# A graph layer with a residual and a norm: 32 instead of 24 hot regions, 1524 instead of 1402 edges a later part, rows weighted in place, sums made part by part

## The chip, the cores and the metric

The kernel runs on one core of a Trainium2 chip. The metric is the device time of one execution in microseconds (us). The kernel before was run three times for its time; a further execution was recorded by the hardware profiler, and all durations of instructions are from that one.

## The reference

A layer of a graph network on 12,500 nodes with 128 features each, and 412,500 edges (200,000 pairs in both directions and one loop at each node), sorted by their target `dst`; all float32:

```python
theta = x[dst] - x[src]
w = jax.nn.sigmoid(jax.nn.relu(theta @ W1 + b1) @ W2 + b2)
agg = jax.ops.segment_sum(w * theta, dst, num_segments=n_nodes)
indeg = jax.ops.segment_sum(jnp.ones((E, 1)), dst, num_segments=n_nodes)
out = _layernorm(x + agg + indeg * (x @ W4 + b4))
```

The sources are random: for each edge a row of 128 floats has to be fetched from a random place. The targets are sorted, so the edges of a part of the list belong to a narrow window of nodes, and a sum by target is a product with a one-hot matrix over that window.

## The kernel before

**Tables.** In 14 chunks (`table_chunk`, L724 to L757) the kernel writes to DRAM the rows z = [x W1 | x] (1 KB a node, by way of buffers `zbuf`) and u = x W4 + b4. The x-rows of a chunk come by way of the buffers `wx`.

**Early parts.** The first 26 parts (`PLAIN`) have 1024 edges each. Every part takes eight indirect gathers of 128 rows (`gather`, L362 to L390, the DMA at L373, issued by POOL; the first eight parts gather from x, the rest from z). POOL carries a short pause between two gathers (`engine_nop`).

**Later parts.** All other edges, 385,876, are cut into 275 parts of 1402 (`CE`) and a tail of 326. Such a part has 1024 gathered slots and 384 hot slots. A hot slot needs no gather: the x-rows of 24 (`HR`) regions of 256 nodes stay in SBUF (`tabs`), each region gives 16 slots a part, and its rows are picked by a product with a one-hot matrix. `place` (L473 to L685) decides which edges of a part become hot: for a set of 64 parts at a time it works on VectorE, region by region, on rows of 702 columns (`WL`) with L548, L552, L553 and L555, and then moves the other edges together in eight steps (L644 to L651). It is a generator: a few of its steps run in each part, as many as a credit allows (`spend`, L1285), beginning some parts before the set is needed. The five sets are 64, 64, 64, 64 and 20 parts; the first is placed during the tables and early parts.

**What a later part does**, with x the source and y the target side:
- PE spreads the target rows: y (L878 in `spread_pair`, for both parts of a block of two), from a one-hot `oh` that ACT makes (L837, L838; `one_hot`, for both parts of a block).
- DVE makes the logits on the gathered rows: subtract (L908), relu times W2 (L913), sum over features (L919), and the one-hot `ow` (L888) by which the sums are made.
- ACT makes the gate by sigmoid (`open_gate`, L925), and again with the counts into the weighted rows (`gate_sums`, L931, L935). DVE weighs four of the eight tiles of 128 rows (L953), ACT the others (L960). The weighted rows go to buffers `wx`, apart from the gathered ones.
- For hot rows, ACT makes the one-hot `of` out of `hot_src` (`hot_tiles`, L996 twice and L998), PE picks the rows (`hot_products`, `pd`, L1010), ACT copies them to `xT` (`hot_out`, L1024). This goes by fetches, each for four regions and eight parts; six fetches serve eight parts (`LEADS`). `hot_rows` (L1043 to L1060) transposes the rows of both parts of a block (L1051), multiplies them by -W1 (L1054) and adds the targets (L1058); DVE makes their logits (L1068), ACT weighs them (L1079), DVE makes their one-hot `owh` (L1083).
- `add_block` (L1121 to L1132) sums both parts of a block at once in PSUM (`pa`, L1101), hot rows too, over a window of 96 nodes (`WB`), and carries the sum on to the next block by a shift matrix (`sh`, L1095, L1096).
- `total`, `finish`, `own` and `normalize` (L1134 to L1200) add the residual and norm the finished rows.

**What sets the order.** In the later parts PE, DVE and ACT run in the order in which the code issues (`IN_ORDER`), written out in `part` (L1363 to L1430). The ring of gather buffers has seven places; part s issues the gathers of part s + 3 (`spread_ahead`, L1356), and the first of the eight waits for the newest PE product issued until then (`paced`), which is one of the part before. SP issues the loads of `hot_src`, window rows and outputs, POOL the gathers.

Of the kernel before, what the change touches and what calls it, by code (L numbers as in the profile page):

```python
# [9 lines left out]
F32 = mybir.dt.float32  # L10
# [10 lines left out]
P = 128  # L21
# [6 lines left out]
WB = 96  # L28
SW = 48
HALF = 64  # L30
AW = 130
G = 4
# [12 lines left out]
HR = 24  # L45
# [7 lines left out]
LEADS = (0, 1, 2, 4, 5, 6)  # L53
NU = 3
# [5 lines left out]
LAST = 121  # L60
LISTS = 2
S2 = P // LISTS
CE = 1402
# [6 lines left out]
PM = 53  # L70
BIG = 1 << 16
STEP = (PM + 1) * HOT
AREA = SW * STEP
# [6 lines left out]
def gnn_resnorm(  # L80
# [46 lines left out]
    assert HOT == 256 and PM == 53 and (HR + 1) * AREA < 1 << 24 and CE % LISTS == 0  # L127
# [165 lines left out]
    def constants():  # L293
# [21 lines left out]
        apart = const.tile([P, PM], F32, name="apart")  # L315
        nc.vector.tensor_scalar(apart, iota_row[:, :PM], float(HOT), None, op0=OP.mult)
# [3 lines left out]
        return nodes, (apart, most, area_c)  # L320


    wx_buf = [const.tile([P, K, AW], F32, name=f"wx{i}") for i in range(NW)]
    wxh_buf = [const.tile([P, SUB * HQ, AW], F32, name=f"wxh{i}") for i in range(2)]
    for t in wxh_buf:
        nc.vector.memset(t[:, :, D + 1:], 1.0)
    xT_all = const.tile([P, HX, HK], F32, name="xT")
# [10 lines left out]
    zbuf = [const.tile([P, K, 2 * D], F32, name=f"zbuf{i}") for i in range(NZ)]  # L338
# [6 lines left out]
    def filled(t, s):  # L345

        if s < NF:
            return t
        return t.rearrange("p (h j) d -> p h j d", h=2)[:, :, :JT, :]

    def rows_of(s):

        if s < NH:
            t = zbuf[s // 2].rearrange("p k d -> p (k d)")[:, (s % 2) * BE:(s % 2 + 1) * BE]
            return t.rearrange("p (k d) -> p k d", d=D)
        return zbuf[(s - NH + NX) % NZ]
# [116 lines left out]
    def place(i, scratch, es, ed, bb, dp):  # L473
# [7 lines left out]
        apart, most, area_c = hot_c  # L481
# [4 lines left out]
        v.tensor_scalar(c[:, 17:18], dp, -float(STEP), float(HR * AREA), op0=OP.mult, op1=OP.add)  # L486
# [17 lines left out]
        nc.scalar.activation(left[:, :HL], ed[:, :HL], AF.Identity, scale=float(STEP), bias=c[:, 17:18])  # L504
# [5 lines left out]
        for j in range(2):  # L510
# [26 lines left out]
        whole = WL // PM * PM  # L537
        v.tensor_tensor(
            left[:, :whole].rearrange("p (a m) -> p a m", m=PM),
            left[:, :whole].rearrange("p (a m) -> p a m", m=PM),  # L540
            apart.rearrange("p (o m) -> p o m", o=1).to_broadcast([P, WL // PM, PM]), op=OP.add)
        if whole < WL:
            v.tensor_add(left[:, whole:], left[:, whole:], apart[:, :WL - whole])
        yield "k"
# [25 lines left out]
        v.tensor_scalar(high, high, HOT.bit_length(), (1 << 13) - 1,  # L570
                        op0=OP.logical_shift_right, op1=OP.bitwise_and)
        v.tensor_scalar(high, high, float(-(-(1 << 16) // ((PM + 1) // 2))), None, op0=OP.mult)
        v.tensor_scalar(high, high, 16, None, op0=OP.logical_shift_right)
# [26 lines left out]
        NC = 4  # L600
        C = -(-WL // NC)
        assert 3 * C <= WL - HKL // 2 and 3 * C < 2 * P * G
        for j in range(NC):
            at = slice(j * C, min(j * C + C, WL))
            m = at.stop - at.start
            pw = scratch()[:, :2 * P * G]
            odd, count, far_on = pw[:, :m + 1], pw[:, C + 1:C + 1 + m], pw[:, 2 * C + 1:2 * C + 1 + m]
# [21 lines left out]
            v.tensor_mul(far_on, count, keep)  # L629
            v.tensor_scalar(keep, far_on, float(LAST), None, op0=OP.is_ge)  # L630
            v.scalar_tensor_tensor(move, keep, -float(P + LAST), far_on, op0=OP.mult, op1=OP.add)
            v.scalar_tensor_tensor(w[:, at], move, 24, w[:, at], op0=OP.logical_shift_left,
# [10 lines left out]
        assert SW + HKL < 2 * LAST and LAST < P - 1 and WL <= 2 * P * G  # L643
        for r, m in enumerate([1 << r for r in range(7)] + [LAST]):  # L644
            u = ep.tile([P, WL], I32, name="et" if r % 2 else "ew")
            bit = scratch().bitcast(I32)[:, :WL]
            v.tensor_scalar(bit, w, 7 - r, 31, op0=OP.logical_shift_left, op1=OP.arith_shift_right)
            v.scalar_tensor_tensor(u, bit, -1, w, op0=OP.bitwise_xor, op1=OP.bitwise_and)
            v.copy_predicated(u[:, :WL - m].bitcast(F32), bit[:, m:], w[:, m:].bitcast(F32))
            yield "m" if r < 7 else "z"  # L650
            w = u  # L651
# [35 lines left out]
    with tc.manual_schedule(engines={SP}), tc.tile_pool(name="work", bufs=2) as wp, tc.tile_pool(  # L687
# [28 lines left out]
        def table_load(c):  # L716
            n0, np_, m = chunks[c]
            xt = wx_buf[c % NW].rearrange("p k d -> p (k d)")[:, :BE]
            xt = xt.rearrange("p (t d) -> p t d", d=D)
            nc.scalar.dma_start(  # L720
                xt[:np_, :m, :], x[n0:n0 + np_ * m, :].rearrange("(p t) d -> p t d", t=m))
            return xt

        def table_chunk(c, xt):  # L724

            n0, np_, m = chunks[c]
            zt = zbuf[NX + c % 3]
# [139 lines left out]
        def spread_pair(b):  # L867

            ys = []
            for h in range(SUB):  # L870
                y = ps_y.tile([P, G, D], F32, name="y")
                parts[b * SUB + h]["y"] = [y]
                ys.append(y)
            for j in range(J):
                for h, y in enumerate(ys):
                    s = b * SUB + h
                    if j < pairs(s):
                        nc.tensor.matmul(y[:, j, :], parts[s]["oh"][:, j * P:(j + 1) * P], y_of(s),  # L878
                                         start=True, stop=True)

        def one_hot_w(s):

            (_, rel, _), i = set_of(s)
            n = pairs(s)
            parts[s]["ow"] = []
            for k0 in range(0, K if s < PLAIN else J, J):
                ow = wp.tile([P, J, WB], F32, name="ow", bufs=4)
                nc.vector.tensor_tensor(  # L888
                    ow[:, :n], iota_f.to_broadcast([P, n, WB]),
                    rel[:, k0:k0 + n, i:i + 1].to_broadcast([P, n, WB]), op=OP.is_equal)  # L890
                parts[s]["ow"].append(ow)

        def logits(s):
# [11 lines left out]
            n = pairs(s)  # L905
            half = h.rearrange("p (i k) d -> p i k d", i=2)[:, :, :n, :]
            yy = y[0][:, :n, :].rearrange("p (o k) d -> p o k d", o=1)
            nc.vector.tensor_sub(half, yy.to_broadcast([P, 2, n, D]), half)  # L908
            w2 = w2_b.rearrange("p (o d) -> p o d", o=1)
            n = K if s < NF else JT  # L910
            tiles = [slice(i, i + n) for i in range(0, K, J if n < K else K)]
            for at in tiles:
                nc.vector.scalar_tensor_tensor(  # L913
                    h[:, at, :], h[:, at, :], 0.0, w2.to_broadcast([P, n, D]),
                    op0=OP.max, op1=OP.mult)
            if s % SUB == 0:
                one_hot_w(s)
            for at in tiles:
                nc.vector.tensor_reduce(lg[:, at, 0], h[:, at, :], AX.X, OP.add)  # L919
            if s % SUB:  # L920
                one_hot_w(s)

        def open_gate(s):

            nc.scalar.activation(filled(gate[:, s % 2].rearrange("p (k e) -> p k e", e=1), s),  # L925
                                 filled(parts[s]["lg"], s), AF.Sigmoid, bias=b2_c)

        def gate_sums(s):

            wx = wx_buf[s % NW]  # L930
            nc.scalar.activation(filled(wx[:, :, D:D + 1], s), filled(parts[s]["lg"], s),  # L931
                                 AF.Sigmoid, bias=b2_c)
# [3 lines left out]

        def weigh(s):

            zs = rows_of(s)
            if s < PLAIN:  # L940
                wx = wx_buf[s % NW]
                for k in range(K):
                    nc.scalar.activation(wx[:, k, :D], zs[:, k, :] if s < NH else zs[:, k, D:],  # L943
                                         AF.Copy, scale=wx[:, k, D:D + 1])
# [3 lines left out]
            if s < NF:  # L948
                xs = zs[:, :KV, D:]
                w, wx = w[:, :KV], wx[:, :KV]  # L950
            else:
                xs, w, wx = filled(zs[:, :, D:], s), filled(w, s), filled(wx, s)
            nc.vector.tensor_tensor(wx, xs, w.to_broadcast(list(xs.shape)), op=OP.mult)  # L953

        def weigh_rest(s):

            if s < NF:
                wx = wx_buf[s % NW]
                for k in range(KV, K):
                    nc.scalar.activation(wx[:, k, :D], rows_of(s)[:, k, D:], AF.Copy,  # L960
                                         scale=wx[:, k, D:D + 1])
# [72 lines left out]
        def hot_y(b, h, q):  # L1034
            return blocks[b]["px"][:, h * P * G + q * P:h * P * G + (q + 1) * P]

        def hot_x(b, i):

            if i < G:
                return pz[:, i * P:(i + 1) * P]  # L1040
            return hot_y(b, i - G, HQ)
# [589 lines left out]
```

## Time and profile before

| | us |
|---|---|
| runs | 3891.53, 3894.61, 3896.50 |
| median | 3894.61 |
| profiled execution | 3877.69 |
| its span, first to last instruction | 3875.8 |
| granted TensorE clock, mean | 0.80 of full |
| one gather of 128 rows on POOL, mean of 2204 | 0.961 |

The profiled execution lies 0.4% below the median; a sum of durations is made against it and then moved to the median.

How to read the lines in the prediction: a row of the timeline is start, duration, engine, line, operation, output and inputs, count, and in brackets how long the engine stood before it and what released it ("remote" where no recorded end fits, "issue" where nothing in the profile was waited for). A row of the groups has the busy time and mean duration in ns behind the bar, then the idle time before these instructions by releaser. A row of the stages has the stretch, its length, and what the text names. PE is TensorE, PEld its weight loads, DVE VectorE, ACT ScalarE, POOL GpSimd, SP SyncE. L12 is line 12 of the kernel before.

### The profile page before, as it was taken

Reading aid. Unit: us, or ns where it says so; the run is one execution under the profiler, and the core shown is the slowest. Engines: PE = TensorE matmul, PEld = TensorE weight load, DVE = VectorE, ACT = ScalarE, POOL = GpSimd, SP = SyncE. Lnnn points to the kernel's source line nnn. Section 1 sums busy time; section 2 is a strip of 40 time slices with the busy share of each in tenths; the row PEclk is TensorE's granted clock in tenths of the full one; section 3 lists DMA queues with packets and bytes.
Section 4 is the critical chain, followed back from the end, with each engine's and each line's share of the span. In section 5 each row is a group of like instructions: output and inputs, shape, how many; then the busy total and the mean of one; then the engine's idle time right before and its main releaser. Section 6 shows DMA issues by size and latency. Waiting matters only on the chain.

```text
span 3875.8 us, 56094 instructions
## 1 busy us (share of the span) xinstructions
PE 2445.5 (63%) x15792; PEld 2080.0 (54%) x15792; DVE 2570.0 (66%) x5694; ACT 2136.0 (55%) x5542; POOL 2324.0 (60%) x2421
## 2 busy tenths in 40 slices
PE   6776566666666666666666666656666666666666
PEld 5555455555555555555555555555555555555555
DVE  6445257777775777777657777776577777765555
ACT  5454455555556555555555555555555555555554
POOL 5544436666666666666666666666666666666663
PEclk9786777778778787878888888788878887788887
DMA  7332224444444444444444434444444444444432
GB/s 265 116 106 76 76 76 112 113 110 115 112 113 120 113 113 113 114 112 112 113 119 113 113 112 111 114 111 112 113 113 112 114 113 114 112 112 112 113 108 71
DMA packets 259988, 437.36 MB, mean 113 GB/s; under 512 B 69817, under 2 KB 177800, under 8 KB 258132
## 3 DMA queue, kind: packets, MB, share of 16 engines
q0 software_dynamic: 114752, 312.11, 28.9%
q1 hardware_dynamic: 142946, 115.19, 11.0%
q10 hardware_dynamic: 1970, 6.40, 0.5%
q8 instruction: 127, 2.08, 0.2%
q14 instruction: 193, 1.58, 0.1%
HBM read 406.12 MB, written 27.33 MB: 112 GB/s over the span
## 4 chain that ended last, share of the span: by engine, by line
DVE 29%; another core or an unknown queue 23%; ACT 16%; issue 15%; PE 13%; POOL 2%; DMA 2%; DVEq 0%; SPq 0%; POOLq 0%; ACTq 0%
DVE zbuf L913 5%; DVE zbuf L908 5%; DVE lg L919 4%; DVE hh L1068 4%; ACT wxh L1079 3%; PE pa L1101 3%; ACT wx L960 3%; ACT of L996 2%; PE pd L1010 2%; POOL zbuf L373 2%; ACT of L998 2%; DVE ow L888 2%; ACT xT L1024 1%; DVE ew L555 1%
## 5 line engine op out<-in xcount | busy, mean ns | idle before, releaser
L373 POOL DMA_INDIRECT zbuf<-z,src_i x2204 | 2117.8, 961 | 1323.7 <-issue 497.2
L1010 PE MATMUL pd<-of,tabs 128*128 128x128 f32 (+1 forms) x3392 | 557.0, 330 | 779.3 <-ACT xT L1024 681.1
L1010 PEld LDWEIGHTS pd<-of,tabs 128*128 128x128 f32 x3392 | 523.6, 242 | 799.2 <-ACT xT L1024 696.5
L1101 PE MATMUL pa<-wx,ow 128*96 128x260 f32 (+1 forms) x2620 | 610.2, 386 | 31.1 <-issue 17.9
L908 DVE TENSOR_TENSOR zbuf<-y,zbuf 128x1024 f32<-128x1024 f32 (+1 forms) x276 | 336.3, 1218 | 338.9 <-remote 275.5
L996 ACT ACTIVATE of<-hot_src,nodes 128x512 f32<-128x512 f16 (+2 forms) x424 | 282.0, 701 | 503.8 <-remote 407.8
L1101 PEld LDWEIGHTS pa<-wx,ow 128*96 128x96 f32 x2620 | 419.1, 172 | 172.1 <-issue 40.0
L953 DVE TENSOR_TENSOR wx<-zbuf,fix 128x512 f32<-128x512 f32 x276 | 189.2, 686 | 399.7 <-ACT fix L925 381.5
L878 PE MATMUL y<-y,oh 64*128 64x128 f32 x2204 | 277.4, 362 | 264.2 <-issue 255.7
L878 PEld LDWEIGHTS y<-y,oh 64*128 64x128 f32 x2204 | 222.5, 252 | 309.0 <-issue 288.1
L960 ACT ACTIVATE wx<-zbuf,wx 128x128 f32<-128x128 f32 x1100 | 349.4, 388 | 0.0
L913 DVE SCALAR_TENSOR_TENSOR zbuf<-zbuf,fix 128x1024 f32<-128x1024 f32 (+1 forms) x277 | 336.5, 1215 | 10.6 <-DVE zbuf L908 0.6
L919 DVE TENSOR_REDUCE lg<-zbuf 128x8 f32<-128x1024 f32 (+1 forms) x277 | 334.7, 1209 | 4.7
L1068 DVE SCALAR_TENSOR_TENSOR hh<-px,w_r 128x128 f32<-128x128 f32 x828 | 240.1, 290 | 139.9 <-remote 113.7
L1054 PE MATMUL px<-wni,xT 128*128 128x128 f32 x1656 | 280.8, 321 | 60.3 <-issue 59.9
L1054 PEld LDWEIGHTS px<-wni,xT 128*128 128x128 f32 x1656 | 260.9, 238 | 68.9 <-issue 68.5
L1024 ACT ACTIVATE xT<-pd 128x512 f32<-128x512 f32 (+7 forms) x347 | 132.0, 415 | 297.5 <-remote 253.3
L1101 PE MATMUL pa<-wxh,owh 128*96 128x130 f32 x1656 | 227.3, 277 | 78.5 <-issue 76.9
L1101 PEld LDWEIGHTS pa<-wxh,owh 128*96 128x96 f32 x1656 | 204.5, 164 | 108.8 <-issue 93.3
L925 ACT ACTIVATE fix<-lg,b_c 128x8 f32<-128x8 f32 (+1 forms) x276 | 74.7, 271 | 325.1 <-issue 179.6
L373 POOL DMA_INDIRECT zbuf<-z,src x144 | 137.6, 955 | 144.3 <-ACT wx L943 98.2
L998 ACT ACTIVATE of<-of 128x1024 f32<-128x1024 f32 (+2 forms) x212 | 219.7, 1036 | 6.5
(266 smaller groups left out, 3885.5 us busy)
## 6 DMA issues: line engine op xcount, KB each, us to landing
zbuf<-z,src_i POOLq DMA_INDIRECT x2204
to_all<-off_d SPq DMA_DIRECT2D x276, 112.0 KB
hot_src<-hot_s SPq DMA_DIRECT2D x182, 128.0 KB
z<-zbuf SPq DMA_DIRECT2D x12, 1024.0 KB
xw<-in_x_dram SPq DMA_DIRECT2D x151, 48.0 KB
u<-u_d SPq DMA_DIRECT2D x151, 48.0 KB
out_dram<-o SPq DMA_DIRECT2D x151, 48.0 KB
y<-z SPq DMA_DIRECT2D x294, 24.0 KB
```

The costliest lines, as they stand in the source:

```text
L373: ins = nc.gpsimd.indirect_dma_start(out=rows_of(s)[:, k, :], out_offset=None, in_=z if s >= NH else x, in_offset=IndirectOffsetOnAxis(ap= ...
L878: nc.tensor.matmul(y[:, j, :], parts[s]["oh"][:, j * P:(j + 1) * P], y_of(s), start=True, stop=True)
L908: nc.vector.tensor_sub(half, yy.to_broadcast([P, 2, n, D]), half)
L913: nc.vector.scalar_tensor_tensor(h[:, at, :], h[:, at, :], 0.0, w2.to_broadcast([P, n, D]), op0=OP.max, op1=OP.mult)
L919: nc.vector.tensor_reduce(lg[:, at, 0], h[:, at, :], AX.X, OP.add)
L960: nc.scalar.activation(wx[:, k, :D], rows_of(s)[:, k, D:], AF.Copy, scale=wx[:, k, D:D + 1])
L996: nc.scalar.activation(of[:, t, :], hot_src[:, i % NU, :w], AF.Abs, bias=nodes[:, t:t + 1])
L998: nc.scalar.activation(of, of, AF.Relu, scale=-1.0, bias=1.0)
L1010: newest[0] = nc.tensor.matmul(to[:, q], tabs[:, g * RG + q, t, :], of[:, t, q], start=t == 0, stop=t == HT - 1)
L1054: nc.tensor.matmul(hot_y(b, h, q), xT[:, h, q * P:(q + 1) * P], wneg, start=False, stop=False, skip_group_check=True)
L1068: nc.vector.scalar_tensor_tensor(h, hot_y(b, *divmod(q, HQ)), 0.0, w2_r, op0=OP.max, op1=OP.mult, accum_out=lg[:, q, :])
L1101: newest[0] = nc.tensor.matmul(to if len(w.shape) == 3 else to[:, 0, :], one, w, start=first and i == 0, stop=last and i == len(terms) - 1)
```

## The change

- A later part has 1524 edges: 1024 gathered slots as before and 512 hot ones of 32 regions. The same edges make 253 full parts and a tail of 304; the sets of `place` are 64, 64, 64 and 62 parts. The tail's sums use the same code as a full part.
- Eight fetches instead of six serve eight parts, one a part; `hot_src` has four buffers instead of three.
- The window of a block is 112 instead of 96 nodes.
- The `wx` buffers go. A row of the gather ring is 260 floats instead of 256, and rows are weighted in place, with the gate and the count behind them. So a place of the ring comes free when PE has summed it. In the table phase the z rows leave from buffers of that pitch.
- Sums are made part by part: `add_part` (s - 1) in part s in place of `add_block`. Hot rows too: `products_ahead` (s + 1, s + 2) makes the hot products of the next part, in one PSUM tile `px`, and the y of the one after.
- In `part` the fetch step stands at the start instead of the end, and a part earlier or later as the diff shows; `one_hot` stands ahead of the logits; the steps of `place` are spent once, at the end of a part, with a credit of 3.0 instead of 2.1.
- `place` has a shorter sort key, without the part number `apart`, 32 rounds, and nine steps of moving in two halves each, on 763 columns.

```diff
-WB = 96
-SW = 48
+WB = 112
+SW = 56
+ZW = 2 * AW
...
-HR = 24
+HR = 32
...
-LEADS = (0, 1, 2, 4, 5, 6)
-NU = 3
+LEADS = (0, 1, 2, 3, 4, 5, 6, 7)
+NU = 4
...
-CE = 1402
+CE = 1524
...
-    wx_buf = [const.tile([P, K, AW], F32, name=f"wx{i}") for i in range(NW)]
...
-    zbuf = [const.tile([P, K, 2 * D], F32, name=f"zbuf{i}") for i in range(NZ)]
+    zbuf = [const.tile([P, K, ZW], F32, name=f"zbuf{i}") for i in range(NZ)]
...
+    def own_of(s):
+        if s < NH:
...
+        return ring(s)[:, :, D:D + AW]
...
-        apart, most, area_c = hot_c
+        most, area_c = hot_c
...
-        for r, m in enumerate([1 << r for r in range(7)] + [LAST]):
...
+        for r in range(MOVES):
+            m = 1 << r
+            u = ep.tile([P, WL], I32, name="ew" if r % 2 else "et")
+            for c0 in range(0, WL, C):
...
         def weigh(s):
...
-            w = gate[:, s % 2].rearrange("p (k e) -> p k e", e=1)
-            wx = wx_buf[s % NW][:, :, :D]
...
+            w = gate[:, s % 2].rearrange("p (k e) -> p k e", e=1)[:, :KV]
+            wx = own_of(s)[:, :KV, :D]
+            nc.vector.tensor_tensor(wx, wx, w.to_broadcast([P, KV, D]), op=OP.mult)
...
+        def products_ahead(s, t):
+            if t < NS:
+                y = ps_y.tile([P, G, D], F32, name="y")
+                parts[t]["y"] = [y]
+            if s < NS:
+                parts[s]["px"] = wide()
+                xT = xT_all[:, (s - PLAIN) % HX, :]
+                for q in range(HQ):
+                    nc.tensor.matmul(hot_x(s, q), xT[:, q * P:(q + 1) * P], ident, start=q == 0,
+                                     stop=False, is_transpose=True, skip_group_check=True)
+                for q in range(HQ):
+                    nc.tensor.matmul(hot_y(s, q), xT[:, q * P:(q + 1) * P], wneg, start=q == 0,
+                                     stop=False, skip_group_check=True)
+            for q in range(max(HQ, J)):
+                if s < NS and q < HQ:
+                    newest[0] = nc.tensor.matmul(
+                        hot_y(s, q), parts[s]["oh"][:, BP + q * P:BP + (q + 1) * P], y_of(s),
+                        start=False, stop=True, skip_group_check=True)
+                if t < NS and q < J:
+                    newest[0] = nc.tensor.matmul(y[:, q, :], parts[t]["oh"][:, q * P:(q + 1) * P], y_of(t),
+                                                 start=True, stop=True)
...
+        def add_part(s):
+            d = parts.pop(s)
+            b, h = divmod(s, SUB)
+            if h == 0:
+                sums_of(b)
+            wx = own_of(s).rearrange("p (h k) d -> p k h d", h=2)
+            terms = [(d["ow"][0][:, k, :], wx[:, k]) for k in range(pairs(s))]
+            terms += [(d["owh"][:, q, :], d["wxh"][:, q, :]) for q in range(HQ)]
+            if h:
+                terms.append((blocks[b]["sh"][:WB, :WB], carry[0][:WB]))
+            products(blocks[b]["pa"], terms, h == 0, h == 1)
...
         def fetch_step(s):
             for f in rest_of:
-                if f[0] - 5 == s:
+                if f[0] - 4 == s:
                     hot_tiles(f)
                     tiled.append(f)
...
         def part(s):
             b, h = divmod(s, SUB)
-            credit[0] = min(credit[0] + 2.1, 5.0)
+            credit[0] = min(credit[0] + 3.0, 6.0)
...
             if opened:
                 hot_out(*opened.pop())
-            if h == 1:
-                advance("c")
+            advance("c")
+            fetch_step(s)
+            if h == 1 and s + 3 < NS:
+                one_hot(s + 3)
             if s < NS:
                 logits(s)
-            spread_ahead(s)
-            if h == 0 and PLAIN // SUB <= b - 1 < NK:
-                add_block(b - 1)
+            if PLAIN + AHEAD <= s + 3 < NS:
+                if s >= PLAIN + 4:
+                    paced[s + 3] = newest[0]
+                gather(s + 3)
+            if PLAIN <= s - 1 < NS:
+                add_part(s - 1)
             if tiled:
-                opened.append((tiled[0], hot_products(tiled.pop())))
-            if h == 1 and b + 1 < NK:
-                spread_pair(b + 1)
-                hot_rows(b + 1)
+                f = tiled.pop()
+                opened.append((f, hot_products(f)))
             if s < NS:
                 open_gate(s)
...
+                hot_logits(s)
+                weigh(s)
+                hot_weights(s)
+                gate_sums(s)
+                one_hot_w(s)
+                weigh_rest(s)
+                products_ahead(s + 1, s + 2)
+            if h == 0 and ended:
+                total(b - 1)
+                finish(b - 1)
+                own(b - 1)
+            if h == 1:
+                if s < NS:
+                    shift(b)
+                if ended:
+                    normalize(b - 1)
+            spend("ksmz")
```

More of the change, by code (lines that the diff above doesn't have):

```diff
@@ L319, in constants @@
                                 op0=OP.mult, op1=OP.add)
-        return nodes, (apart, most, area_c)
-    wx_buf = [const.tile([P, K, AW], F32, name=f"wx{i}") for i in range(NW)]
-    wxh_buf = [const.tile([P, SUB * HQ, AW], F32, name=f"wxh{i}") for i in range(2)]
+        return nodes, (most, area_c)
+    wxh_buf = [const.tile([P, HQ, AW], F32, name=f"wxh{i}") for i in range(2)]
     for t in wxh_buf:
         nc.vector.memset(t[:, :, D + 1:], 1.0)
+    xt_buf = [early(BE) for _ in range(NW)]
     xT_all = const.tile([P, HX, HK], F32, name="xT")
@@ L726, in table_chunk @@
             n0, np_, m = chunks[c]
[L727 removed]
+            zt = zbuf[NX + c % 3][:, :, :2 * D]
             us = us_buf[c % 2]
@@ L1428, in gnn_resnorm @@
+            spend("ksmz")
         with tc.manual_schedule(engines=IN_ORDER):
-            for s in range(PLAIN, NS + 4):
+            for s in range(PLAIN, NS + 2):
                 part(s)
```

269 lines of the change are left out of this document (78 added, 191 removed).

## The prediction

> **What bounds the kernel now.** I read the page first, then the span by stage (busy time of each engine, and the start of each later part's first VectorE step, L908), then the timeline of POOL, PE, ACT and DVE around 2,700 us, then the groups by shape.
>
> The page and the stages:
>
> ```profile
> PE 2445.5 (63%) x15792; PEld 2080.0 (54%) x15792; DVE 2570.0 (66%) x5694; ACT 2136.0 (55%) x5542; POOL 2324.0 (60%) x2421
> ...
> 0.00:115.00 115.00, 77.23 (x524) 62.09 (x524) 80.42 (x216) 60.74 (x112) 68.61 (x73) 0.98 0.78 271
> 117.00:520.00 403.00, 266.18 (x1470) 203.08 (x1468) 152.04 (x350) 189.01 (x452) 190.08 (x200) 0.74 0.30 86
> 524.00:3858.00 3334.00, 2091.22 (x13753) 1806.61 (x13751) 2329.62 (x5095) 1879.42 (x4958) 2064.85 (x2148) 0.80 0.41 111
> 1100.00:1300.00 200.00, 125.52 (x835) 109.11 (x834) 138.88 (x304) 113.72 (x304) 125.68 (x132) 0.81 0.42 117
> 3600.00:3800.00 200.00, 127.14 (x816) 109.30 (x816) 108.89 (x241) 109.73 (x297) 122.89 (x130) 0.80 0.39 109
> ...
> 1100.00:1300.00 200.00, 19.51 (x16) 0.81 0.42 117
> 3600.00:3800.00 200.00, 19.49 (x16) 0.80 0.39 109
> ...
> L908 DVE TENSOR_TENSOR zbuf<-y,zbuf x5: 1212/1217/1226, 523.9 to 559.2; 128x1024 f32<-128x1024 f32 x5
> ...
> L908 DVE TENSOR_TENSOR zbuf<-y,zbuf x4: 680/1218/1225, 3830.8 to 3856.6; 128x1024 f32<-128x1024 f32 x3, 128x512 f32<-128x512 f32 x1
> ```
>
> Columns of the stages: PE, PEld, DVE, ACT, POOL busy, PE clock, DMA share, GB/s; of the two short rows: L908 alone. No engine is full. Parts run from 523.9 to 3856.6: 275 intervals of 12.12 us, 86% of the span; tables and plain parts take the first 524. The reader is to see that DVE falls from 138.88 to 108.89 us of 200 when `place` has ended, and that as many parts start. DVE's load does not set the rate.
>
> What does, POOL shows:
>
> ```profile
> 2698.10 0.94 POOL L373 DMA_INDIRECT zbuf<-z,src_i  x1 [2.20 <-remote]
> ...
> 2706.84 0.95 POOL L373 DMA_INDIRECT zbuf<-z,src_i  x1 [0.30 <-issue]
> 2711.13 0.94 POOL L373 DMA_INDIRECT zbuf<-z,src_i  x1 [3.34 <-PE px L1058]
> 2712.38 0.95 POOL L373 DMA_INDIRECT zbuf<-z,src_i  x1 [0.30 <-issue]
> ...
> 2719.89 0.94 POOL L373 DMA_INDIRECT zbuf<-z,src_i  x1 [0.30 <-issue]
> 2723.07 0.95 POOL L373 DMA_INDIRECT zbuf<-z,src_i  x1 [2.24 <-remote]
> ...
> 2734.88 0.94 POOL L373 DMA_INDIRECT zbuf<-z,src_i  x1 [2.11 <-remote]
> ...
> 2700.78 3.78 PE L1010 MATMUL pd<-of,tabs 128*128 128x128 f32 x16 [11.61 <-ACT xT L1024]
> ...
> 2708.75 0.27 PE L1054 MATMUL px<-wni,xT 128*128 128x128 f32 x1 [0.45 <-issue]
> ...
> 2709.89 0.94 PE L1058 MATMUL px<-y,oh 64*128 64x128 f32 x12
> ...
> 2715.90 1.95 PE L1010 MATMUL pd<-of,tabs 128*128 128x128 f32 x16
> ...
> 2720.46 0.27 PE L878 MATMUL y<-y,oh 64*128 64x128 f32 x1 [1.18 <-issue]
> ```
>
> A part's eight gathers follow each other every 1.25 us: from 2711.13 to 2719.89 + 0.94 a run takes 9.70 us. Then POOL stands 2.1 to 3.3 us until the PE product arrives by which the next part's gathers are paced (`paced`, L1356). Starts of runs: 2698.10, 2711.13, 2723.07, 2734.88, thus 13.03, 11.94 and 11.81 us. That is the clock of the kernel: **a run of 9.7 us and one answer of PE**. The second thing to see is when the answer comes. The `pd` products end by record at 2717.85, the run that is paced by the end of that part's products starts at 2723.07, and "remote" says that no recorded end fits: the signal was seen only after the run had ended at 2720.83. So in this stretch a product's signal that is not given early in a run reaches the others only when the run is over. PE, DVE and ACT then make one round per run, with time to spare inside it.
>
> **The change part by part.** *Fewer gathers.* The 385,876 edges of the later parts are cut into 253 full parts and a tail of 304 instead of 275 and 326. A part has 1024 gathered slots as before and 512 hot ones instead of 384; 22 runs go. At 12.12 us this is 267 us (6.9%), and all that the change can bring. It keeps this only as far as a part does not get longer: with 253 intervals against 275, a part may grow by 8%.
>
> *What a part gains in work.* The rows:
>
> ```profile
> L908 DVE TENSOR_TENSOR zbuf<-y,zbuf 128x1024 f32<-128x1024 f32 x275 | 335.6, 1220 | 338.9 <-remote 275.5 <-PE px L1054 24.2 <-PE y L878 21.2
> L919 DVE TENSOR_REDUCE lg<-zbuf 128x8 f32<-128x1024 f32 x275 | 334.0, 1214 | 4.7
> ...
> L996 ACT ACTIVATE of<-hot_src,nodes 128x512 f32<-128x512 f16 x398 | 268.5, 711 | 486.8 <-remote 395.1 <-PE pd L1010 36.0 <-PE px L1054 32.6
> L1068 DVE SCALAR_TENSOR_TENSOR hh<-px,w_r 128x128 f32<-128x128 f32 x828 | 240.1, 290 | 139.9 <-remote 113.7 <-PE pa L1101 1.8
> ...
> L998 ACT ACTIVATE of<-of 128x1024 f32<-128x1024 f32 x199 | 210.3, 1057 | 6.3
> ...
> L953 DVE TENSOR_TENSOR wx<-zbuf,fix 128x512 f32<-128x512 f32 x275 | 188.5, 686 | 399.7 <-ACT fix L925 381.5 <-issue 10.8 <-ACT xT L1024 7.4
> L1079 ACT ACTIVATE wxh<-pz,wxh 128x128 f32<-128x128 f32 x552 | 157.5, 368 | 4.5
> L837 ACT ACTIVATE oh<-to_all,away,mine 128x896 f32<-128x896 bf16 x136 | 152.2, 1119 | 0.0
> L888 DVE TENSOR_TENSOR ow<-fix,rel 128x384 f32<-128x384 f32 x275 | 151.0, 549 | 0.0
> ...
> L1083 DVE TENSOR_TENSOR owh<-fix,hrel 128x576 f32<-128x576 f32 x138 | 103.4, 749 | 0.0
> ...
> L552 DVE MAX8 ed<-ew 128x8 f32<-128x702 f32 x96 | 85.3, 889 | 2.1
> L555 DVE MATCH_REPLACE8 ew<-ed,ew 128x702 f32<-128x702 f32 x96 | 83.8, 873 | 0.0
> L548 DVE SCALAR_TENSOR_TENSOR ew<-ew 128x702 f32<-128x702 f32 x92 | 81.5, 886 | 1.8
> ...
> L1024 ACT ACTIVATE xT<-pd 128x512 f32<-128x512 f32 x65 | 38.2, 588 | 100.4 <-remote 87.7 <-PE px L583 8.5 <-PE y L878 4.3
> ```
>
> DVE. Without `place` a part costs 108.89 / 200 x 12.12 = 6.6 us. Added: a fourth hot tile in L1068 (0.29 + its reading of the sum, some 0.08), `ow` by 112/96 (+0.09), `owh` of 448 instead of 288 elements a part (0.61 against 0.37 by its row's ns an element). Sum +0.7: **7.3 us**. `place`: all later parts cost DVE 2329.6 / 276 = 8.44, less 6.6 is 1.84 x 276 = 508 us, 127 for each of four sets (16 of them short). After it there are 32 rounds instead of 24 of L548, L552, L555 (2.65 us, on 763 columns instead of 702: 2.88; 92 against 64, +28); the other 63 us grow by 763/702 and by a ninth move, less the key's `apart`; estimate 170 a set, three sets, each spread by a credit of 3.0 a part over some 48 parts: **3.5 us in 144 of the 254 parts**, so 10.8 us there.
>
> ACT. One `hot_tiles` every part instead of three in four (two L996 and one L998, 2.5 us), four `hot_weights` (L1079, at most 0.37 each) for three, `one_hot` of 1024 columns instead of 896. Busy 113.72 / 200 x 12.12 = 6.9 us goes to about 8.2. It isn't full, but the order counts: `hot_tiles`, and in every second part `one_hot` (L837 1.12 x 1024/896, its second step estimated near it: 2.4), now stand ahead of `open_gate`, for which DVE's L953 already waits 381.5 us. The weighing in place costs nothing (same instructions, another target); the ring has seven buffers and part s+3 gets that of s-4, which PE has summed two parts earlier, so the new release is hidden by the ring. If not, it would show as a POOL wait on L1101.
>
> PE. 50 recorded matmuls a part (an f32 product counts two, a transpose one) become 61: 16 `pd` for 12, 8 `y` as before, 12 for 9 in the hot rows' transposes and `wneg` products, 8 for 6 with `oh`, 8 `pa` of the sums as before, 8 for 6 of the hot sums, 1 shift. At 2091.22 / 276 = 7.6 us a part this goes to 9.2: below a run of 9.7, but all of it falls between the answers.
>
> SP gets eight instead of six `hot_src` loads in eight parts, four buffers for three; POOL's queue order is as before. Both are taken at nothing: DMA share 0.41.
>
> *The loop of a part after.* A restart at 0; DVE and ACT get what PE had finished. ACT: `hot_out` 0.6 (L1024) and `hot_tiles` 2.5, the gates some 0.6, with `one_hot` 2.4 more; DVE meanwhile logits (L908, L913, L919, 3.7) and four hot tiles 1.5; `hot_weights` end between 5.2 and 7.6. The hot rows now have one `px`, so PE may start the next part's 28 products only then. They need 28 x 0.12 = 3.4 us at the spacing of the 16 `pd` of 2715.90, 28 x 0.24 = 6.6 at that of 2700.78. They end at 8.6 to 14.2, the run at 9.7. Where they end before 9.7, the answer is seen some 2.2 after the run, T = 11.9; at the late end T = 14.2 and a signal. A gain per part I exclude: the run of 9.7 and an answer of 2.1 stand in every cycle. I take **T = 12.5**, midway between the ordinary cycle of before (11.9) and that of 2698.10 to 2711.13 (13.03), in which PE, after 11.61 us of standing for ACT's `hot_out`, issued 62 matmuls, as many as a part has after; I am nearer to neither.
>
> *Ahead of it.* Two more tables and fetches of some 3.1 us on ACT, a longer first `place`, and a z store whose rows in SBUF no longer touch, so 1 KB pieces instead of 8 KB, at a DMA share of 0.78: estimate +20 us (from -30, if the early parts hide it in their 15.5 us a part, to +60).
>
> *Sum.* 523.9 + 20 + 253 x 12.5 (3162.5) + 19.2 from the last L908 to the span's end + 1.9 around the span = 3727.5, against 3877.69 of the profiled execution (span 3875.8). That execution lies 16.9 us below the median of the runs; so **3745 us**. Each 0.1 us of T is 25 us; the break-even is T = 13.09.
>
> **The rivals.**
> *PE's issue stalls in every cycle (13.0).* In the cycle from 2698.10 PE issued matmuls one at a time from 2708 on (0.45 us of issue ahead of 2708.75; 1.18 ahead of 2720.46 in the next), though nothing that it read was late. The first such stall comes after some 50 matmuls of a cycle. 50 a part mostly fit below that; 61 don't. Then every cycle is 13.03: 523.9 + 20 + 3296.6 + 21.1 + 16.9 = 3879, 0.4% under before. For it: the two stalls. Against: the cycle with the longer stall took 11.94 only. [...]
>
> *Slower: `place` in the loop of `px`.* If in a placing part DVE's 3.5 us and its 3.7 us of logits stand between the seen signal and `hot_logits`, then the loop is 3.5 + 3.7 + 1.5 + 0.3 + 1.4 on DVE and ACT, 3.4 to 6.6 on PE and some 0.5 of signals: 14.3 to 17.5; I take 14.5, since PE's clock was 0.80 to 0.81 in these stages. With 144 such parts and 109 intervals of 12.5 the mean is 13.64: 523.9 + 20 + 3450.5 + 21.1 + 16.9 = 4032 (the last terms are 19.2 + 1.9 and the step to the median). It decides from 13.54 in the placing parts on. For it: the hot tiles of both parts of a block were one round before and are two now, and 10.8 us of DVE leave 1.7 for 2.7 us of waits (338.9 + 399.7 over 275). Against: `place` moved the rate by nothing so far, and logits need only `y`, which is made a part earlier than `px`.
>
> *The rate isn't the gathers' at all.* If a part's time goes by its slots (PE, ACT and DVE together), T = 12.12 x 1536/1408 = 13.22: 523.9 + 20 + 3344.7 + 21.1 + 16.9 = 3927. Against it: the same rate at 138.88 and 108.89 us of DVE.
>
> **How the numbers follow.** Forecast (T 12.0 to 12.9, 3618 to 3846) 0.52; stalls in every cycle 0.16 (3846 to 3900); `place` in the loop 0.25 (3890 to 4060); by slots 0.07 (3927). Measured differences under 0.2% (7.8 us) can't be told from none. Faster: 0.52 and 0.11 of the stalls, 0.63; same 0.04 (3887 to 3902, mostly of the stalls); slower 0.33. Eight in ten lie in 3640 to 4010; the forecast's own range is 3640 to 3846.
>
> **What would show it.** Right: L908 every 12.3 to 12.7 us, 16 a window in 200 us, 2028 gathers in the later parts, POOL's gap 2.2 to 3, and as many parts with as without `place`. PE's stalls: gaps of 3.3 throughout, PE rows of one product with "issue". `place` in the loop: intervals of 14 or more that drop to 12.5 when `place` has ended, L1068's counterpart late behind DVE, POOL waiting for PE `px` products over 4 us. By slots: 13.2 everywhere. A POOL wait on sums of PE, or a first later part past 600 us, would make the prediction wrong elsewhere.

## The result and the profile after

The changed kernel took 3730.36 us (median of 4 runs, 3721.54 to 3737.03) beside 3893.82 us for the kernel before on the same chip: a ratio of 0.958, 95% interval 0.9557 to 0.9600. The forecast was 3745 us. That holds where the kernel before takes 3890 us. On three other chips the kernel before takes 3160 us; on one of them the changed kernel was run too, unaltered, and takes 1.65% longer (experiment 4).

The profiled execution of the changed kernel took 3721.54 us, its span was 3719.8. First the page, then the stages; the columns are those of the stages before (PE, PEld, DVE, ACT, POOL, PE clock, DMA share, GB/s):

```profile
PE 2778.9 (75%) x17515; PEld 2330.1 (63%) x17515; DVE 2608.9 (70%) x6043; ACT 2316.0 (62%) x5830; POOL 2138.8 (57%) x2245
```

```profile
700.00:900.00 200.00, 141.66 (x1012) 120.79 (x1012) 178.97 (x389) 135.75 (x344) 128.88 (x134) 0.93 0.44 119
...
1900.00:2100.00 200.00, 138.96 (x855) 117.41 (x854) 108.54 (x260) 112.28 (x288) 104.37 (x111) 0.80 0.38 103
...
2900.00:3100.00 200.00, 157.83 (x963) 133.43 (x962) 117.47 (x265) 124.66 (x324) 120.07 (x127) 0.82 0.42 115
```

The first subtraction of each later part, now L889, in those stages (its busy time and count), and its first and last starts:

```profile
700.00:900.00 200.00, 19.50 (x16) 0.93 0.44 119
...
1900.00:2100.00 200.00, 17.12 (x14) 0.80 0.38 103
...
2900.00:3100.00 200.00, 19.60 (x16) 0.82 0.42 115
```

```profile
L889 DVE TENSOR_TENSOR zbuf<-y,zbuf x6: 1215/1216/1225, 513.8 to 575.0; 128x1024 f32<-128x1024 f32 x6
```

```profile
L889 DVE TENSOR_TENSOR zbuf<-y,zbuf x4: 1217/1220/1225, 3664.9 to 3699.0; 128x1024 f32<-128x1024 f32 x4
```

From 513.8 to 3699.0 lie 253 intervals of 12.59 us, where before there were 275 of 12.12. The reader is to see two things. DVE goes from 178.97 to 117.47 us of 200 and the same 16 parts start: here too its load doesn't set the rate. And one stage, 1900 to 2100, has 14.

The timeline of POOL, at the same place as before:

```profile
2704.40 0.95 POOL L376 DMA_INDIRECT zbuf<-z,src_i  x1 [0.30 <-issue]
2708.26 0.94 POOL L376 DMA_INDIRECT zbuf<-z,src_i  x1 [2.92 <-PE y L1023]
...
2717.01 0.94 POOL L376 DMA_INDIRECT zbuf<-z,src_i  x1 [0.30 <-issue]
2720.98 0.94 POOL L376 DMA_INDIRECT zbuf<-z,src_i  x1 [3.02 <-PE y L1023]
...
2729.73 0.95 POOL L376 DMA_INDIRECT zbuf<-z,src_i  x1 [0.30 <-issue]
2733.18 0.94 POOL L376 DMA_INDIRECT zbuf<-z,src_i  x1 [2.51 <-PE y L1023]
...
2746.85 0.94 POOL L376 DMA_INDIRECT zbuf<-z,src_i  x1 [3.97 <-PE y L1023]
```

And PE in the second of these cycles:

```profile
2717.14 0.38 PE L1019 MATMUL px<-y,oh 64*128 64x128 f32 x2
2719.03 0.27 PE L1023 MATMUL y<-y,oh 64*128 64x128 f32 x1 [1.51 <-issue]
2719.78 0.36 PE L1023 MATMUL y<-y,oh 64*128 64x128 f32 x1 [0.48 <-issue]
...
2720.31 0.39 PE L1023 MATMUL y<-y,oh 64*128 64x128 f32 x1
2720.63 3.53 PE L1060 MATMUL pa<-zbuf,ow 128*112 128x260 f32 x8
```

A run is 9.69 us as before. PE stops at 2717.5, issues two of its last products one at a time, and goes on without stops only at 2719.78, 1.8 us after the run has ended at 2717.95. The last product of the part ends at 2720.70, and POOL goes on at 2720.98. The gap, 2.1 to 3.3 us in the cycles shown of before, is 2.5 to 4.0 in these. Over all gaps between runs from 560 us on its mean goes from 2.43 to 2.89 us, so by 0.46, as the part did (12.12 to 12.59); without the long stop told below to 2.79. PE stops for over 0.3 us on "issue" in 222 of 241 cycles of the changed kernel, and in 170 of 249 before (counted from 600 us on).

The stage with 14 parts holds one thing that the prediction did not have. SP's queue and ACT there:

```profile
2002.76 0.71 SPq L181 DMA_DIRECT2D es<-in_src_dram  x2
2003.79 6.04 SPq L184 DMA_DIRECT2D es<-in_src_dram  x1
2009.93 9.62 SPq L181 DMA_DIRECT2D ed<-in_dst_dram  x2
2019.60 10.02 SPq L184 DMA_DIRECT2D ed<-in_dst_dram  x1
...
2030.59 7.00 SPq L191 DMA_DIRECT2D dp<-in_dst_dram  x1
...
2038.36 2.65 SPq L191 DMA_DIRECT2D dp<-in_dst_dram  x1
2041.12 0.82 SPq L948 DMA_DIRECT2D hot_src<-hot_s  x2
```

```profile
2048.88 1.24 ACT L834 ACTIVATE oh<-to_all,away,mine 128x1024 f32<-128x1024 bf16 x1 [27.71 <-DMA to_all<-off_d]
```

SP issues the loads of `place`'s last set for 38 us, from 2002.76 to 2041.01. In the kernel before, those of its last set took from 2753.60 to 2761.06:

```profile
2753.60 0.59 SPq L182 DMA_DIRECT2D es<-in_src_dram  x2
2754.24 0.30 SPq L185 DMA_DIRECT2D es<-in_src_dram  x1
...
2760.77 0.29 SPq L192 DMA_DIRECT2D dp<-in_dst_dram  x1
```

Behind these loads stand those that the next block needs, so ACT waits 27.7 us for `to_all`. One interval, from 2012.65 on, is 42.0 us long.

### The profile page after: what moved, and what is told of

Same layout as the page of the kernel before. It is cut to its first block, busy times and chain, and to the rows that moved or that the text cites. A ratio compares the mean times of both kernels' runs of the same rounds, so it can differ in the third digit from the quotient of the medians.

```text
span 3719.8 us, 60470 instructions
## 1 busy us (share of the span) xinstructions
PE 2778.9 (75%) x17515; PEld 2330.1 (63%) x17515; DVE 2608.9 (70%) x6043; ACT 2316.0 (62%) x5830; POOL 2138.8 (57%) x2245
## 3 DMA queue, kind: packets, MB, share of 16 engines
q1 hardware_dynamic: 164060, 126.53, 12.6%
## 4 chain that ended last, share of the span: by engine, by line
PE 38%; ACT 18%; issue 17%; DVE 15%; another core or an unknown queue 6%; DMA 3%; POOL 1%; SPq 1%; DVEq 0%; POOLq 0%; ACTq 0%
PE pa L1060 14%; PE pd L973 6%; PE px L1019 4%; PE px L1015 3%; PE y L1023 3%; ACT zbuf L912 3%; ACT of L959 3%; ACT wxh L1040 2%; DVE zbuf L891 2%; DMA zbuf<-z,src_i 2%; DVE zbuf L889 2%; DVE lg L892 2%; PE px L1012 2%; DVE hh L1031 2%
## 5 line engine op out<-in xcount | busy, mean ns | idle before, releaser
L1060 PE MATMUL pa<-zbuf,ow 128*112 128x260 f32 (+1 forms) x2444 | 831.9, 497 | 83.0 <-issue 48.3
L1060 PEld LDWEIGHTS pa<-zbuf,ow 128*112 128x112 f32 x2444 | 534.5, 241 | 278.8 <-issue 118.6
L1023 PE MATMUL y<-y,oh 64*128 64x128 f32 x2032 | 430.2, 333 | 240.7 <-issue 235.3
L973 PE MATMUL pd<-of,tabs 128*128 128x128 f32 (+3 forms) x4176 | 526.8, 280 | 74.1 <-ACT of L961 56.4
L1019 PE MATMUL px<-y,oh 64*128 64x128 f32 x2032 | 409.1, 325 | 196.9 <-issue 196.1
L1023 PEld LDWEIGHTS y<-y,oh 64*128 64x128 f32 x2032 | 323.3, 220 | 293.6 <-issue 293.0
L921 DVE TENSOR_TENSOR zbuf<-zbuf,fix 128x512 f32<-128x512 f32 x254 | 174.2, 686 | 340.0 <-ACT fix L896 168.5
L912 ACT ACTIVATE zbuf<-zbuf 128x128 f32<-128x128 f32 x1224 | 389.1, 390 | 0.4
L1060 PEld LDWEIGHTS pa<-wxh,owh 128*112 128x112 f32 x2032 | 330.0, 217 | 42.5 <-issue 2.7
L1060 PE MATMUL pa<-wxh,owh 128*112 128x130 f32 x2032 | 326.7, 313 | 0.6 <-issue 0.6
L889 DVE TENSOR_TENSOR zbuf<-y,zbuf 128x1024 f32<-128x1024 f32 x254 | 310.1, 1221 | 24.2 <-DMA zbuf<-z,src_i 12.2
L891 DVE SCALAR_TENSOR_TENSOR zbuf<-zbuf,fix 128x1024 f32<-128x1024 f32 x254 | 310.2, 1221 | 17.5
L892 DVE TENSOR_REDUCE lg<-zbuf 128x8 f32<-128x1024 f32 x254 | 309.8, 1220 | 8.7
```

The source lines that it names most:

```text
L889: nc.vector.tensor_sub(half, yy.to_broadcast([P, 2, J, D]), half)
L891: nc.vector.scalar_tensor_tensor(h, h, 0.0, w2.to_broadcast([P, K, D]), op0=OP.max, op1=OP.mult)
L892: nc.vector.tensor_reduce(lg[:, :, 0], h, AX.X, OP.add)
L912: nc.scalar.activation(wx[:, k, :D], wx[:, k, :D], AF.Copy, scale=wx[:, k, D:D + 1])
L973: newest[0] = nc.tensor.matmul(to[:, q], tabs[:, g * RG + q, t, :], of[:, t, q], start=t == 0, stop=t == HT - 1)
L1019: newest[0] = nc.tensor.matmul(hot_y(s, q), parts[s]["oh"][:, BP + q * P:BP + (q + 1) * P], y_of(s), start=False, stop=True, skip_group_ch ...
```

## The experiments

The experiments were made in four groups (the expectations say "calls"), each on one chip, with the kernel before beside the others. What "before" took tells which kind of chip it was. In a group an altered kernel was run once.

**1. First group (before: 3159.71 us).** The four expectations were worked out for a chip on which before takes 3890 us.

`few_edges`: 1402 edges a part.

```diff
-CE = 1524
+CE = 1402
```

> The changed kernel with 1402 edges a part as before, everything else of the change kept: 276 later parts instead of 254, each with slots left empty. Theory (the gain is the fewer parts alone, and a part got 0.5 us longer): 275 intervals of 12.6 us, about 4000 us, 2.7% above the kernel before. Rival (the new order, the weighing in place and the part-by-part sums bring time by themselves): below 3894 us, near 3750 us if they bring all of it.

It took 3449.76 us, 9.2% above before on that chip, and 276 parts of 11.08 us in the mean. Neither number came: the time is that of another kind of chip. What it does show is that, on that chip, the rest of the change brings nothing by itself: with the same number of parts as before it costs 290 us. That rest is more than order, weighing in place and sums part by part, since `few_edges` keeps the 32 regions too, with their rounds of `place` and their hot products; which of these costs how much was not separated.

`six_gathers_after` leaves out two of eight gathers of a later part, from the ninth later part on:

```diff
         for k in slots(s):
+            if PLAIN + 8 <= s < NF and k % J == J - 1:
+                continue
```

> The changed kernel leaves out two of the eight gathers of each later part (those two tiles keep old rows). Theory (a part is its run of gathers and one answer of PE): the run falls from 9.7 to 7.2 us, a part from 12.6 to about 10.2, 3120 us. Rival (a round through PE, ACT and DVE of 12.6 us sets the part, the gathers lie beside it): 3700 to 3730 us. Between the two: the share of the 2.5 us that goes tells how much slack the round has.

3131.00 us, against 3216.96 of the whole changed kernel on another such chip (experiment 4): 2.7% less. Stretches with `place` kept 12.0 to 12.3 us a part, those without went from 10.0 to 8.9. On that chip the gathers set the part only where `place` doesn't run.

`pd_twice_after` makes the hot picks twice:

```diff
-            for q in range(RG):
+            for q in [q for q in range(RG) for _ in range(2)]:
```

> The changed kernel makes the products that pick hot rows twice (the second time over the first, same values): 77 instead of 61 recorded matmuls a part. If PE's issue within a run is what made a part longer than before (12.0 to 12.6): 16 more at 0.12 to 0.24 us each and the stalls, 2 to 4 us a part, 4200 to 4700 us. If PE has room inside the run: under 0.5 us a part, below 3860 us.

3246.18 us, 0.9% above 3216.96. About half of the difference lies ahead of the later parts, which begin at 397.6 us instead of 382.8; the mean part goes from 11.12 to 11.17 us. So 16 more recorded matmuls cost some 0.04 us a part, and on that chip PE has room.

`pace_early_after`:

```diff
-                    nc.tensor.matmul(hot_y(s, q), xT[:, q * P:(q + 1) * P], wneg, ...
+                    mark[0] = nc.tensor.matmul(hot_y(s, q), xT[:, q * P:(q + 1) * P], wneg, ...
...
-                    paced[s + 3] = newest[0]
+                    paced[s + 3] = mark[0]
```

> The changed kernel paces a run of gathers by the last wneg product of the part before instead of by its last y product, 16 recorded matmuls later. Theory (PE's last products are issued late, and the run of gathers waits for them): a gap of 2.2 instead of 2.9 us, 11.9 to 12.1 us a part, 3560 to 3620 us. Rival (PE's stalled products must wait for the end of a run in any case; an earlier run then holds them up longer): no gain or slower, 3730 to 3900 us.

3216.20 us: nothing against 3216.96.

**2. Second group (before: 3889.66 us, 7 runs): the kind of chip of the result.**

> The changed kernel, nothing altered, beside the kernel before on the chip of this call. In the first call the kernel before took 3160 us, not 3894. If that chip gives PE's signals while gathers run, then before is bound by its gathers (10.0 us a part) and the changed kernel, at 12.2 us where place runs (48 parts of each of three sets) and 10.0 elsewhere, takes about 3210 us, 1.5% slower than before. On a chip like that of the result: 3730 against 3894 us. Rival (the chip is only faster in all it does): the ratio of 0.958 holds on both.

3723.15 us (4 runs), ratio 0.958, interval 0.9558 to 0.9603; 12.56 us a part. The result came again.

> The kernel before, nothing altered, for its trace on this chip. If it takes near 3160 us: runs of gathers back to back with no gap of 2.4 us between parts, no PE matmuls issued one at a time at the end of a run, 10.0 to 10.2 us a part whether place runs or not. If near 3894 us: the trace known.

3891.68 us, 12.13 us a part, with POOL's gaps of 2.2 and 3.2 us as in the first trace.

`pd_twice_before` is the same edit of `hot_products` as above, in the kernel before.

> The kernel before makes the products that pick hot rows twice: 62 instead of 50 recorded matmuls a part, as many as the changed kernel has. If PE's load is what makes a part longer (12.1 to 12.6 on the chip of the result): there about 4030 us, 3.5% over before. If the part by part loop does it: within 0.5% of before. Where gathers bind with 10.0 us a part: within 0.5% of before as well.

4136.54 us, 6.3% above before, more than expected; 12.99 us a part instead of 12.13. The timeline of POOL shows where:

```profile
2712.48 0.95 POOL L373 DMA_INDIRECT zbuf<-z,src_i  x1 [0.30 <-issue]
2715.80 0.95 POOL L373 DMA_INDIRECT zbuf<-z,src_i  x1 [2.37 <-remote]
...
2724.57 0.95 POOL L373 DMA_INDIRECT zbuf<-z,src_i  x1 [0.30 <-issue]
2732.33 0.95 POOL L373 DMA_INDIRECT zbuf<-z,src_i  x1 [6.81 <-PE px L1058]
```

A run of eight keeps its length (2715.80 to 2724.57 + 0.95: 9.72 us); the gap behind a run in which PE had more to do grows, here to 6.81 us. With no change in order, buffers, `place` or number of parts, more matmuls alone make the part longer. This is the step "what a part gains in work, PE" by itself, and it speaks against the part by part loop as the only cause of 12.59. The sizes differ, though: 12 more matmuls cost 0.86 us a part here, and the change, with 11 more, 0.47. Picks made twice also end later for ACT, which copies them (some 2 us, an estimate from 16 more recorded matmuls at the 0.12 us of the 16 `pd` of 2715.90), so the count of matmuls alone doesn't give the length.

`six_gathers_before` is the edit of `six_gathers_after` in the kernel before.

> The kernel before leaves out two of the eight gathers of each later part (those tiles keep old rows). Where the part is a run of gathers and one answer of PE: 2.5 us less a part, 3220 us beside 3894, or on the other chip 7.5 us a run, so that another engine takes over near 9 us a part: about 2850 beside 3160. If a round of PE, ACT and DVE sets it: no change.

3262.69 us, 16.1% less, near the 3220 of the theory; a part takes 9.85 us, 2.28 less. The timeline of POOL has runs of six and gaps much like those before (mean 2.56 against 2.41 us in `before_again`):

```profile
2301.35 0.94 POOL L375 DMA_INDIRECT zbuf<-z,src_i  x1 [2.15 <-remote]
...
2307.60 0.95 POOL L375 DMA_INDIRECT zbuf<-z,src_i  x1 [0.30 <-issue]
2312.24 0.95 POOL L375 DMA_INDIRECT zbuf<-z,src_i  x1 [3.69 <-PE px L1060]
...
2318.49 0.95 POOL L375 DMA_INDIRECT zbuf<-z,src_i  x1 [0.30 <-issue]
2321.39 0.95 POOL L375 DMA_INDIRECT zbuf<-z,src_i  x1 [1.95 <-remote]
```

So PE's answer moves forward with the end of the run. It isn't a round of fixed length beside the gathers: on this chip a part is its run and the answer behind it.

**3. Third group (before: 3159.12 us).** Two kernels of the first group once more.

> The changed kernel with 1402 edges a part, once more, if possible on a chip on which the kernel before takes near 3890 us. Theory (the fewer parts bring the gain, the part itself got 0.5 us longer): 275 intervals of 12.6 us, about 3995 us, 2.7% above before. Rival (order, weighing in place and sums part by part bring time): below 3890 us. Where before takes 3160 us: 3450 us as in the first call.

> The changed kernel with runs of gathers paced by the last wneg product of the part before, 16 recorded matmuls earlier, once more beside before at 3890 us if possible. Theory (PE's last products of a part are issued only when a run has ended, and the next run waits for them): gap 2.2 instead of 2.9 us, about 3560 to 3620 us. Rival (the held-up products then fall into the next run and are held up by that): 3730 us or more. Where before takes 3160 us: 3216 us as in the first call.

3449.51 and 3220.63 us: the times of the first group again. What the two edits do on the kind of chip of the result was not measured.

**4. Fourth group (before: 3163.58 us, 7 runs).**

> The changed kernel, nothing altered, once more. On chips where the kernel before takes 3160 us the changed one hasn't run yet: place's 12.0 to 12.4 us a part in some 150 parts and 10.0 in the others, as the altered kernels of the first call showed, give 3200 to 3230 us, a ratio of 1.01 to 1.02. Where before takes 3890 us: 3725 us, 0.958.

3216.96 us (4 runs, 3214.76 to 3220.93), ratio 1.0165, interval 1.0148 to 1.0182: under 2%, but clear of the spread of the runs, and as worked out from the first group. The stages of this trace, as above, L889 by itself behind them, then POOL and PE where `place` has ended:

```profile
1100.00:1300.00 200.00, 145.35 (x1014) 128.99 (x1015) 178.36 (x383) 136.32 (x347) 134.21 (x139) 0.85 0.46 122
2700.00:2900.00 200.00, 160.97 (x1220) 142.83 (x1220) 145.02 (x342) 160.93 (x410) 151.25 (x161) 0.93 0.53 144
```

```profile
1100.00:1300.00 200.00, 19.50 (x16) 0.85 0.46 122
...
2700.00:2900.00 200.00, 24.49 (x20) 0.93 0.53 144
```

```profile
2707.71 1.95 PE L973 MATMUL pd<-of,tabs 128*128 128x128 f32 x16
2710.17 0.66 PE L1012 MATMUL px<-wni,xT 128*128 128x128 f32 x4 [0.51 <-ACT wxh L1040]
```

```profile
2706.99 0.95 POOL L376 DMA_INDIRECT zbuf<-z,src_i  x1 [0.30 <-issue]
2708.24 0.95 POOL L376 DMA_INDIRECT zbuf<-z,src_i  x1 [0.30 <-issue]
2709.49 0.94 POOL L376 DMA_INDIRECT zbuf<-z,src_i  x1 [0.30 <-issue]
```

With `place` 16 parts start in 200 us and DVE is busy 89% of it; without, 20 parts, and POOL gathers every 1.25 us with no gap at a part's end: 8 x 1.25 = 10.0 us. While those gathers flow, ACT sees PE's products and PE sees ACT's answer within the run (0.51 us of waiting at 2710.17). The group of the y products shows the stops gone in one number, the trace of the result first, then that of this chip (us of PE's idle time before L1023, and how many times):

```profile
  issue: 528.3, 517
```

```profile
  issue: 0.2, 1
```

The kernel is the same, with 17515 recorded matmuls in either trace.

> The changed kernel with runs paced by the last wneg product of the part before, beside the changed kernel itself on one chip. Where before takes 3890 us: theory (the next run waits for PE's last products only) 3560 to 3620 us; rival (the held-up products are held up by the earlier run as well) 3730 us or more. Where before takes 3160 us, place and the gathers set the part and pacing has room: within 10 us of the changed kernel.

3217.99 us, 1 us from the changed kernel: here pacing has room. Of the versions that do the whole work, none that was run is faster than the kernel before on this kind of chip.

## Why the prediction was right, and where it wasn't

**The clock of the kernel** (run of 9.7 us and one answer of PE): right on the chip of the result, shown by `six_gathers_before`. But it belongs to that kind of chip: on the three others before is 731 us faster, and in the trace of experiment 4 PE's signals are seen while gathers run, so that where `place` doesn't run there is no answer to wait for. Before was not traced there; (3159.7 - 377.9 - 23.7) / 275 = 10.0 us a part is an estimate, with start and end taken from `few_edges`, and it is the length of eight gathers. The prediction had no means to see this, as its only trace came from one chip. What differs is open.

**Fewer gathers**: 22 x 12.12 = 267 us, as forecast. The part took back 253 x 0.47 = 119 us of it; the first part came 10 us earlier; 156 us are left in the profiled executions (3877.69 to 3721.54). This split is worked out from the two traces; no run on this kind of chip had the change with 1402 edges a part.

**T = 12.5**: measured 12.59, and 12.47 without the one interval of 42.0. The midpoint was a choice, not a derivation; so that it came this near is in part luck. Its reason, that PE's last products come late when it has 61 matmuls a part, is what the POOL gaps show and `pd_twice_before` supports, with another size. The loop through the single `px` was not separated from it.

**`place` at nothing** on this chip: right (16 parts at 178.97 and at 117.47 us of DVE). The parts without `place` were even a little longer (mean from start to start 12.68 us in 2900 to 3100, 12.10 in 700 to 900), with PE's clock at 0.82 instead of 0.93. The two go together; which follows from which wasn't tried.

**Ahead of it, +20**: wrong in sign, 523.9 went to 513.8, inside the range given. The z rows do leave in smaller pieces: of the DMA packets 1856 have 8 KB and more in the execution before, 338 in the one after.

**Weighing in place at nothing**: right by the rows. In either trace the median is 687 ns for DVE's four tiles (L953, now L921) and 387 for a tile on ACT (L960, now L912).

**SP's loads at nothing**: wrong. The loads of the last set held SP's queue for 38 us and cost one part 29 us. The prediction counted the sets' parts but did not ask how SP loads a last set of 62 parts. It is not a matter of the chip: in the fourth group's trace four of these loads take 7.3 to 10.1 us and one interval is 45.2, while `few_edges`, whose last set has 20 parts, has no load of `place` over 1.1 us and no interval over 15.1. Why the four take 6 to 10 us is open.

**The step to the median**, 16.9 us, was 8.8. With T (+23), the start (-30) and this (-8), the terms miss 3745 by 15 us; they are mis-sized in both directions, and that the sum is so near is partly luck. (The prediction's 0.61 us for `owh` is 0.58 by the row that it names; its sum of 0.7 stands.)

**The rivals.** "PE's issue stalls in every cycle" was half true: the stalls came in 222 of 241 cycles, at 12.6 and not at 13.0 us. The number of matmuls does not give them alone: with the same 17515 recorded matmuls the fourth group's trace has 0.2 us of issue before the y products against 528.3. What makes PE stop is not shown. "By slots" (13.22) fell. "`place` in the loop" fell on this chip and is what happens on the others, by a simpler way than its loop. DVE's timeline in the fourth group's trace, from one part's first step to the next's, and its one stop in the part after:

```profile
703.91 1.23 DVE L889 TENSOR_TENSOR zbuf<-y,zbuf 128x1024 f32<-128x1024 f32 x1 [0.20 <-issue]
...
715.31 0.94 DVE L550 MATCH_REPLACE8 ew<-ed,ew 128x763 f32<-128x763 f32 x1
716.16 1.21 DVE L889 TENSOR_TENSOR zbuf<-y,zbuf 128x1024 f32<-128x1024 f32 x1
...
724.31 0.29 DVE L1106 TENSOR_TENSOR a<-a,pa 112x130 f32<-112x130 f32 x1 [1.55 <-ACT a L1098]
```

This part of 12.25 us has no marked idle time of DVE in the rows left out; in the next DVE stands 1.55 us once, for ACT. Its work is what the prediction had counted: in the stretch from 1100 to 1300, with 12.05 us a part, 178.36 / 200 x 12.05 = 10.7 us against 10.8. DVE as the limit of these parts fits experiment 1: neither two gathers less (12.0 to 12.3 us) nor more picks (0.04 us a part in the mean of all) change them, and in `few_edges`, whose rows of `place` have 702 columns instead of 763, they take 11.8 to 12.1 us instead of 12.0 to 12.3. On those chips the fewer parts bring 233 us (3449.6 to 3217.0), and the rest of the change costs 290.

## What to carry to other kernels

Ask what the part waits for, then what a change does to that wait: fewer parts pay by the length of a part, and lose what each part gains in length on the resource that is waited for (here 22 x 12.12 us and 253 x 0.47). Here a wait for signals that come later than the recorded end of their instruction (5.2 us in the case below) stood on one kind of chip and not on another; measure on a second chip before a balance of DVE, PE and gathers is tuned to it. When the number of sets changes, look at the loads of the last, partial one.

## What the runs showed of the hardware

One kernel, unaltered, took 3160 us on three chips, and 3890 us on the chip of the second group and where the result was measured. Each chip that the record names was measured on one occasion, so the chip can't be told from the occasion. Where it takes 3890 us, matmuls are issued one at a time, 0.5 to 1.5 us apart in the cycle shown, late in a run of indirect gathers and until some 1.8 us after its end; before the y products of the changed kernel such stops come to 528.3 us in the trace of the result, 549.0 in that of the second group and 0.2 in that of the fourth. In the kernel before a signal of PE is seen 5.2 us after its recorded end (2717.85 to 2723.07), when the run has ended (2720.83). The trace's own records of semaphores bear that out: PE's products end at 2716.06 and 2717.85, but between 2710.87 and 2722.65 no update by PE stands in it, and then two do, at 2722.65 and 2722.81. Where `place` doesn't run, a part of the changed kernel needs 10.0 us in the fourth group where it needs 12.7 on the chip of the result.

The traces of the two kinds differ in one thing more. For the same changed kernel that of the result holds 21184 records of semaphore updates, that of the fourth group 66918. So records are missing there, or several stand as one, and what ended a wait, "remote" and "issue" above all, is less certain in those traces. Every run listed here has a recorded span and clock, so it isn't excluded that recording itself holds the engines up on the one kind. No run here says why the kinds differ.
